# Attention's scores and values in four 64x64 tiles of the array, with two accumulators for the values

## The chip, the cores and the metric

The kernel runs on one core of a Trainium2 chip. The metric is the device time of one execution in microseconds (us). The kernel before has a median of 3139.4 us over three runs, from 3138.46 to 3145.35.

Engines are named as the profile names them: PE (TensorE, matmuls), PEld (its weight loads), DVE (VectorE), ACT (ScalarE), POOL (GpSimd) and SP (the queue that issues most transfers). All arithmetic is in float32.

## The reference, cut to what matters

An image batch x of shape (4, 128, 64, 64) passes through two layers. Layer 0 adds to x a group-normed block of three convolutions (7x7, 5x5, 3x3) and a non-local attention. Layer 1 is a two-way state-space block (mamba) and a recurrence. The change touches the attention of layer 0 only:

```python
g_x = conv1x1(x, gw, gb).reshape(B, IC, hw)      # IC = 64, hw = 4096
theta = conv1x1(x, tw, tb).reshape(B, IC, hw)
phi = conv1x1(x, pw, pb).reshape(B, IC, hw)
f = jnp.einsum('bcn,bcm->bnm', theta, phi) / jnp.sqrt(jnp.float32(IC))
attn = jax.nn.softmax(f, axis=-1)
out = jnp.einsum('bcm,bnm->bcn', g_x, attn)
out = conv1x1(out.reshape(B, IC, H, W), ow, ob)
```

Each of the four images has 4096 queries and 4096 keys of 64 channels.

## The kernel before, in words

`conv_attention` runs layer 0. It takes the queries in 32 tiles of 512 (eight for each image; `n` in the loop), and for each tile it does two things one after the other on PE: a chunk of attention, and a piece of the convolutions (`convolve`, whose matmuls are `products`, L367).

**The attention chunk.** The keys of an image are 32 blocks of 128, kept in pairs. `phi` holds channels of even blocks on partitions 0 to 63 and of odd blocks on 64 to 127; the queries `th` are held twice, once on each half. The loop over `i` has 8 steps of four key blocks. In a step:

- `scores` (L460, L462) takes two pairs. For each pair one PSUM tile `pf` of two banks is filled by two matmuls with 64 rows and 128 columns of the array, one for each half of the partitions (`HALF[e]`) into a bank of its own. ScalarE takes the exponential of both banks in one instruction into `ex` (four buffers).
- `values` (L471) multiplies each `ex` with the transposed `gT`: 128 rows, 64 columns, even blocks into the lower half of the accumulator `acc`, odd ones into the upper half. VectorE adds `ex` into `es` (L475, L477), for the denominators.

On PE the scores of step i+1 stand ahead of the values of step i, so a tile's order is two steps of scores, then values and scores in turn, then two steps of values. PE and ACT run in an order written out by hand; DVE, POOL and SP take their instructions in the order of dependencies that the program gives.

**After the chunk.** VectorE adds the two halves of `es` (L651). The convolution's first products go into PSUM tiles of the pool `ps_c`, which has three banks that go round, and are evicted by ACT (L410) and DVE (L414, L418, L420). After the first eviction comes `divide`: a matmul with ones gives the denominators `den` (L481), VectorE inverts them into `att` (L483), takes their extremes for a guard (L484, L485) and multiplies `acc` by them (L486). `collect` (L491, L493) projects finished tiles and adds them to the image. Before the convolution's last products `queries` (L449, L451) makes the next `th`, and the next tile's scores follow.

[...]

**Other work within the chunk.** `making_forms` prepares the convolution's inputs on POOL and ACT (L298, L337, L347); in the first two tiles `making` prepares the convolution's weights on VectorE (L537 to L582); `late` holds additions to the image on POOL (L388, L501). They are issued step by step between scores and values.

Of the kernel before, what the change touches and what calls it, by code (L numbers as in the profile page):

```python
# [10 lines left out]
F32 = mybir.dt.float32  # L11
AF = mybir.ActivationFunctionType
ALU = mybir.AluOpType
AX = mybir.AxisListType
PSUM = bass.MemoryType.PSUM

P = 128
NC = 512
# [130 lines left out]
def run(parts):  # L149
    for _ in parts:  # L150
        pass


def conv_attention(nc, tc, k, a, t, B, H, W, flags, load, mem, loads):
# [17 lines left out]
    NT = T // P  # L172
# [14 lines left out]
    with ExitStack() as ctx:  # L187
# [15 lines left out]
        HALF = [slice(0, IC), slice(IC, P)]  # L203
# [15 lines left out]
        wk = ctx.enter_context(tc.tile_pool(name="l0_wk", bufs=2))  # L219
# [4 lines left out]
        ps_v = ctx.enter_context(tc.tile_pool(name="l0_v", bufs=1, space=PSUM))  # L224
        ps_c = ctx.enter_context(tc.tile_pool(name="l0_c", bufs=3, space=PSUM))
# [7 lines left out]
        dmax = wp.tile([1, B * NQ], F32, name="dmax")  # L233
        dmin = wp.tile([1, B * NQ], F32, name="dmin")

        def statistics(b):

            st = wk.tile([P, NQ, nc.vector.BN_STATS_DIM], F32, tag="st", name="st")
            for j in range(NQ):
                nc.vector.bn_stats(st[:, j, :], t[:, ds(b * T + j * NC, NC)])  # L240
            mv = wk.tile([P, 2], F32, tag="mv", name="mv")
            nc.vector.bn_aggr(mv, st)
            pm = ps_c.tile([P, 1], F32, tag="c", name="pm")
            nc.tensor.matmul(pm, k.gmean, mv[:, 0:1], start=True, stop=True)
            gm = wk.tile([P, 1], F32, tag="gm", name="gm")
            nc.vector.tensor_copy(gm, pm)
            dm = wk.tile([P, 1], F32, tag="dm", name="dm")
            nc.vector.tensor_tensor(dm, mv[:, 0:1], gm, ALU.subtract)
            qv = wk.tile([P, 1], F32, tag="qv", name="qv")
            nc.vector.scalar_tensor_tensor(qv, dm, dm, mv[:, 1:2], ALU.mult, ALU.add)  # L250
            pv = ps_c.tile([P, 1], F32, tag="c", name="pv")
            nc.tensor.matmul(pv, k.gmean, qv, start=True, stop=True)
            ve = wk.tile([P, 1], F32, tag="ve", name="ve")
            nc.vector.tensor_scalar(ve, pv, GN_EPS, None, ALU.add)
            rs = wk.tile([P, 1], F32, tag="rs", name="rs")
            rsqrt(nc, k, rs, ve)
            return gm, rs
# [25 lines left out]
        def rows(b, r0, r1):  # L283

            nc.vector.tensor_scalar(
                xp[:, 3 + r0 : 3 + r1, 3 : 3 + W],
                t[:, ds(b * T + r0 * W, (r1 - r0) * W)].rearrange("p (h w) -> p h w", w=W),
                *gn[b], ALU.subtract, ALU.mult,
            )
# [80 lines left out]
        def fetch(m, n):  # L370
            wt = fm.tile([P, 9, P], F32, tag="wt", name="wt")
            nc.scalar.dma_start(wt, wd[3 * m + n])
            return wt
# [71 lines left out]
        def queries(n):  # L445
            b, q = divmod(n, NQ)
            pt = ps_c.tile([P, NC], F32, tag="c", name="pt")
            r = 3 + q * RW
            nc.tensor.matmul(pt, tw, xp[:, r : r + RW, 3 : 3 + W], start=True, stop=True)  # L449
            th = wk.tile([P, NC], F32, tag="theta", name="theta", bufs=1)  # L450
            nc.scalar.activation(th, pt, AF.Identity, bias=tb2)  # L451
            return th

        def scores(th, m0):

            out = []
            for m in range(2 * m0, 2 * m0 + 2):
                pf = ps_f.tile([P, 2, NC], F32, tag="f", name="pf")
                for e in range(2):
                    nc.tensor.matmul(pf[:, e, :], phi[HALF[e], m, :], th[HALF[e]], start=True, stop=True)  # L460
                ex = ep.tile([P, 2, NC], F32, tag="ex", name="ex")
                nc.scalar.activation(ex, pf, AF.Exp, scale=scale)  # L462
                out.append(ex)
            return out

        def values(m0, exs, acc, es):

            for i, ex in enumerate(exs):
                m = 2 * m0 + i
                for e in range(2):  # L470
                    nc.tensor.matmul(  # L471
                        acc[HALF[e]], gT[:, 2 * m + e, :], ex[:, e, :], start=(m == 0), stop=(m == NT // 2 - 1)
                    )
                if m == 1:
                    nc.vector.tensor_tensor(es, exs[0], ex, ALU.add)  # L475
                elif m > 1:
                    nc.vector.tensor_tensor(es, es, ex, ALU.add)  # L477

        def divide(n, acc, es):
            den = ps_c.tile([P, NC], F32, tag="c", name="den")  # L480
            nc.tensor.matmul(den, k.ones, es[:, 0, :], start=True, stop=True)  # L481
            att = wk.tile([P, NC], F32, tag="att", name="att", bufs=4)
            nc.vector.reciprocal(att, den)  # L483
            nc.vector.tensor_reduce(dmax[:, n : n + 1], att[0:1, :], AX.X, ALU.max)  # L484
            nc.vector.tensor_reduce(dmin[:, n : n + 1], att[0:1, :], AX.X, ALU.min)  # L485
            nc.vector.tensor_tensor(att, acc, att, ALU.mult)  # L486
            return att

        def collect(n, att):
# [105 lines left out]
        phi = big.tile([P, NT // 2, P], F32, name="phi")  # L595
        gT = big.tile([P, NT, IC], F32, name="gT")
        gn, mid, atts, xl, late, begun = {}, {}, {}, [], {}, set()
# [9 lines left out]
        def product(n):  # L607
            b, q = divmod(n, NQ)
            return (FIRST if b == 0 else ORDER if b + 1 < B else LAST)[q]

        th = None
        for j in range(T // XT):
            part = keys(0, j)
            next(part)
            if j == T // XT - 1:
                th = queries(0)
# [10 lines left out]
        for n in range(N):  # L627
            b, q = divmod(n, NQ)
            more = b + 1 < B and q == NQ - 1
            if 3 <= n < B + 2:  # L630
                load(n - 2)
            m, f, wts = product(n), nf, None
            if b + 1 < B and q == NQ - 3:
                gn[b + 1] = statistics(b + 1)
            if more:
                rows(b + 1, 0, H)
            acc = ps_v.tile([P, NC], F32, tag="v", name="acc")
            es = ep.tile([P, 2, NC], F32, tag="es", name="es", bufs=1)
            for i in range(NB):
                exs = nxt  # L640
                if i + 1 < NB:
                    nxt = scores(th, i + 1)
                values(i, exs, acc, es)
                next(making_forms, None)
                next(making, None)
                if m < 6 and i == NB - 3:
                    wts = [fetch(m, 0), fetch(m, 1)]
                due = late.get(n, [])
                for _ in range(-(-len(due) // (NB - i))):
                    due.pop(0)()  # L650
            nc.vector.tensor_tensor(es[:, 0, :], es[:, 0, :], es[:, 1, :], ALU.add)  # L651

            for i, _ in enumerate(convolve(n, b, m, f, wts)):
                if i == 0:

                    if q not in ((1, 2, 3) if b == 0 else (1,)):
                        for o in sorted(atts):
                            collect(o, atts.pop(o))
                    if q == 0 and n:
                        finish(b - 1)  # L660
                    if n == N - 1:
                        load_last()
                if i == 1:
                    atts[n] = divide(n, acc, es)
                if i == 2 and n + 1 < N:

                    nf = []
                    making_forms = forms(product(n + 1), nf)
                    next(making_forms, None)
                if more and i < T // XT:  # L670
                    part = keys(b + 1, i)
                    next(part)
                if i == 2 and n + 1 < N:
                    th = queries(n + 1)
                if i == 3 and n == NQ + 5:
                    mr = wk.tile([P, NT, 2], F32, tag="mr", name="mr", bufs=1)
                    stats = row_scales(nc, k, ps_c, "c", wk, t[:, 0:T], mr, mem)
                if i == 3 and n >= NQ + 5:
                    next(stats, None)
                if more and i < T // XT:  # L680
                    run(part)
                if i == 4 and n == N - 1:
                    collect(n, atts.pop(n))
                    finish_last(0)
            if n + 1 < N:
                nxt = scores(th, 0)
# [1070 lines left out]
```

## Time and profile before

| | us |
|---|---|
| median of three runs | 3139.4 |
| span of the profiled execution | 3147.0 |
| PE busy in it | 2925.4 |
| DVE busy | 2195.2 |
| ACT busy | 1813.8 |
| POOL busy | 1798.5 |
| L460 scores, PE, 2048 records | 513.6 |
| L471 values, PE, 2048 records | 492.8 |
| L477 additions to `es`, DVE, 448 | 683.2 (1.525 each) |
| L462 exponentials, ACT, 512 | 497.6 (1.021 each) |

The page gives the span, from the first instruction to the last, and no other time of that execution. Busy time is the time in which at least one record of a kind ran. PE's records overlap: the mean length of a score record is 0.619 us, while 513.6 us over 2048 records are 0.25 us each. So lengths of records say little about PE's pace, and one reads the distance from start to start instead. A line of the timeline gives the start, the length, the engine, the line, the operation with out<-in, rows*columns of the array, the shape and the count of merged records; in brackets stands the idle time before it and what ended it.

Attention and convolution take the stretch to about 1643 us; the granted clock of PE is 1.00 on average from 105 us to there, and 0.977 over the whole span, where it falls to half for stretches of 3.4 us and more.

### The profile page before, as it was taken

What the parts mean: (1) busy time and instruction counts of PE and PEld (TensorE: products, weight loads), DVE (VectorE), ACT (ScalarE), POOL (GpSimd) and SP (SyncE); (2) the same over time, 40 slices, a digit from 0 to 9 for tenths busy, and PEclk for the clock granted to TensorE, in tenths of its full rate; (3) what the DMA queues carried; (4) which work ended last, traced back from release to release, by engine and by line L of the source; (5) the groups of instructions that cost most, each with busy time, mean ns of one, the idle gap of its engine ahead of it and who ended that gap; (6) DMA issues with size and microseconds to landing.
All of it is one profiled execution on the core that took longest, in us unless ns stands there. A gap on an engine that the chain in (4) does not pass through costs nothing. (4 is left out here: it accounts for less than half of the span.)

```text
span 3147.0 us, 42863 instructions
## 1 busy us (share of the span) xinstructions
PE 2925.4 (93%) x15511; PEld 1458.2 (46%) x15511; DVE 2195.2 (70%) x3429; ACT 1813.8 (58%) x3102; POOL 1798.5 (57%) x1393
## 2 busy tenths in 40 slices
PE   6799999999999999999997999999999999999976
PEld 1344444454444454444453444444444444455545
DVE  7876668666777667687765767776677766777667
ACT  3343434433444434444434878887788778888756
POOL 4258448456584665766553565565555565565644
PEclk9999999999999999999998999999999999999988
DMA  5310101010100101010023343334333343333332
GB/s 181 133 39 30 38 31 45 8 43 23 46 23 30 43 23 38 31 52 33 11 74 92 91 117 95 98 95 115 82 100 94 80 120 89 105 95 103 87 109 109
DMA packets 108394, 224.16 MB, mean 71 GB/s; under 512 B 25678, under 2 KB 29390, under 8 KB 106764
## 3 DMA queue, kind: packets, MB, share of 16 engines
q1 hardware_dynamic: 96588, 177.53, 19.9%
q10 hardware_dynamic: 11584, 43.78, 4.1%
q8 instruction: 125, 2.05, 0.3%
q14 instruction: 97, 0.79, 0.1%
HBM read 200.83 MB, written 20.44 MB: 70 GB/s over the span
## 5 line engine op out<-in xcount | busy, mean ns | idle before, releaser
L477 DVE TENSOR_TENSOR es<-es,ex 128x1024 f32<-128x1024 f32 x448 | 683.2, 1525 | 139.2 <-ACT ex L462 105.8
L462 ACT ACTIVATE ex<-pf 128x1024 f32<-128x1024 f32 x512 | 497.6, 1021 | 464.7 <-PE pf L460 421.2
L460 PE MATMUL pf<-theta,phi 64*128 64x512 f32 x2048 | 513.6, 619 | 20.4 <-ACT ex L462 20.0
L471 PE MATMUL acc<-ex,gT 128*64 128x512 f32 x2048 | 492.8, 607 | 1.7 <-ACT ex L462 1.7
L1202 POOL TENSOR_TENSOR ct<-ct,Cst 128x512 f32<-128x512 f32 x128 | 170.7, 1334 | 343.6 <-DMA ct<-csmem 314.1
L460 PEld LDWEIGHTS pf<-theta,phi 64*128 64x128 f32 x2048 | 173.0, 185 | 340.0 <-ACT ex L462 172.3
L1168 ACT ACTIVATE lt<-lt,cs 128x128 f32<-128x128 f32 x1024 | 312.1, 390 | 0.5 <-DMA lt<-csmem 0.5
L367 PE MATMUL pm<-yf,wt 128*128 128x256 f32 x1152 | 287.1, 382 | 11.9 <-DVE att L483 11.0
L410 ACT ACTIVATE eo<-pm 128x256 f32<-128x256 f32 x88 | 33.7, 383 | 448.9 <-PE pm L367 442.3
L471 PEld LDWEIGHTS acc<-ex,gT 128*64 128x64 f32 x2048 | 127.9, 137 | 339.8 <-issue 327.8
L367 PEld LDWEIGHTS pm<-yf,wt 128*128 128x128 f32 x1152 | 212.9, 189 | 93.4 <-issue 38.7
L1103 PE MATMUL pb<-tl,wbc_fwd 128*64 128x512 f32 x512 | 241.9, 616 | 6.5 <-DVE xT L1135 6.5
L1103 PE MATMUL pb<-tl,wbc_bwd 128*64 128x512 f32 x512 | 242.5, 617 | 0.0
L337 POOL TENSOR_TENSOR yf<-yd 128x272 f32<-128x272 f32 x192 | 234.0, 1246 | 1.4
L1267 POOL TENSOR_TENSOR yT<-yT,zT 128x512 f32<-128x512 f32 x127 | 166.5, 1316 | 58.1 <-DVE yT L1254 50.0
L337 POOL TENSOR_TENSOR yf<-xp 128x272 f32<-128x272 f32 x128 | 108.7, 880 | 136.0 <-PE pm L367 130.2
L1201 DVE TENSOR_TENSOR lt<-lt,gm 128x1024 f32<-128x1024 f32 x128 | 179.2, 1400 | 1.9
L1135 DVE SCALAR_TENSOR_TENSOR xT<-px,taps_bwd,xT 128x512 f32<-128x512 f32 x192 | 143.7, 748 | 8.7 <-ACT xT L1129 4.0
L1234 PE MATMUL y<-lt,xdt 128*64 128x128 f32 x2048 | 142.3, 282 | 7.6 <-PE ptr L1177 3.8
L1221 POOL TENSOR_TENSOR S<-S,tot 128x256 f32<-128x256 f32 x120 | 91.4, 762 | 100.7 <-PE y L1242 91.2
L1103 PEld LDWEIGHTS pb<-tl,wbc_fwd 128*64 128x64 f32 x512 | 66.9, 141 | 174.3 <-issue 142.9
L367 PE MATMUL pm<-yf,wc 128*128 128x256 f32 x512 | 131.3, 384 | 6.6 <-DVE att L483 5.1
(297 smaller groups left out, 5655.5 us busy)
## 6 DMA issues: line engine op xcount, KB each, us to landing
lt<-csmem SPq DMA_DIRECT2D x128, 512.0 KB, 5.7
wt<-wd ACTq DMA_DIRECT2D x72, 576.0 KB, 3.8
ct<-csmem SPq DMA_DIRECT2D x256, 128.0 KB, 5.2
rs<-m SPq DMA_DIRECT2D x31, 512.0 KB, 3.8
wd<-t SPq DMA_DIRECT2D x16, 576.0 KB, 2.8
t<-in_x SPq DMA_DIRECT2D x4, 2048.0 KB, 11.0
rows<-after SPq DMA_DIRECT2D x32, 256.0 KB, 4.4
out<-t SPq DMA_DIRECT2D x4, 2048.0 KB, 14.4
```

The lines of the kernel that those rows point to most:

```text
L337: nc.gpsimd.tensor_tensor(f[:, kx], at(x), at(y), op)
L367: nc.tensor.matmul(pm[:, e, :], wt, src, start=(i == 0), stop=(i == len(terms) - 1))
L460: nc.tensor.matmul(pf[:, e, :], phi[HALF[e], m, :], th[HALF[e]], start=True, stop=True)
L462: nc.scalar.activation(ex, pf, AF.Exp, scale=scale)
L471: nc.tensor.matmul(acc[HALF[e]], gT[:, 2 * m + e, :], ex[:, e, :], start=(m == 0), stop=(m == NT // 2 - 1))
L477: nc.vector.tensor_tensor(es, es, ex, ALU.add)
L1103: nc.tensor.matmul(out, w[i]["bc"][:, tap, bass.ts(c, DS)], src, start=(tap == 0), stop=(tap == KC - 1),)
L1135: nc.vector.scalar_tensor_tensor(at(n), px, taps[:, PAD - n : KC - n], at(n), ALU.mult, ALU.add)
L1168: nc.scalar.activation(v, v, AF.Relu, scale=-1.0, bias=m["b"]["cs"][:, d, m["i"], h : h + 1])
L1201: nc.vector.tensor_tensor(lt, lt, gm.unsqueeze(2).to_broadcast([P, ND, NHEAD, P]), ALU.mult)
L1202: nc.gpsimd.tensor_tensor(m["ct"], m["ct"], Cs[:, cols].unsqueeze(1).to_broadcast([P, NHEAD, P]), ALU.mult)
L1267: eng.tensor_tensor(v, v, gr["z"][d][:, :, half(d, j // 2)], ALU.mult)
```

## The change

The scores' matmuls are split by output: each of the two becomes two of 64 rows and 64 columns, one for each half of the keys in a block (`c`), so that four matmuls fill `pf` on the four quarters of the array.

The values' matmuls are split by operand: the lower and the upper half of a key block's partitions (`r`) go into different accumulators, `acc[0]` in `ps_v` and `acc[1]`, a new tile in one of the three banks of `ps_c`. Both are held for the whole chunk. At its end ScalarE copies `acc[1]` to `att` in SBUF and VectorE adds `acc[0]` to it. `divide` gets this sum; it puts the inverted denominators into the second half of `es`, which is free by then.

```diff
-                for e in range(2):
-                    nc.tensor.matmul(pf[:, e, :], phi[HALF[e], m, :], th[HALF[e]], start=True, stop=True)
+                for c in HALF:
+                    for e in range(2):
+                        nc.tensor.matmul(pf[c, e, :], phi[HALF[e], m, c], th[HALF[e]], start=True, stop=True)
...
                 for e in range(2):
-                    nc.tensor.matmul(
-                        acc[HALF[e]], gT[:, 2 * m + e, :], ex[:, e, :], start=(m == 0), stop=(m == NT // 2 - 1)
-                    )
+                    for r in range(2):
+                        nc.tensor.matmul(
+                            acc[r][HALF[e]], gT[HALF[r], 2 * m + e, :], ex[HALF[r], e, :],
+                            start=(m == 0), stop=(m == NT // 2 - 1),
+                        )
...
-        def divide(n, acc, es):
+        def divide(n, att, es):
             den = ps_c.tile([P, NC], F32, tag="c", name="den")
             nc.tensor.matmul(den, k.ones, es[:, 0, :], start=True, stop=True)
-            att = wk.tile([P, NC], F32, tag="att", name="att", bufs=4)
-            nc.vector.reciprocal(att, den)
-            nc.vector.tensor_reduce(dmax[:, n : n + 1], att[0:1, :], AX.X, ALU.max)
-            nc.vector.tensor_reduce(dmin[:, n : n + 1], att[0:1, :], AX.X, ALU.min)
-            nc.vector.tensor_tensor(att, acc, att, ALU.mult)
+            r = es[:, 1, :]
+            nc.vector.reciprocal(r, den)
+            nc.vector.tensor_reduce(dmax[:, n : n + 1], r[0:1], AX.X, ALU.max)
+            nc.vector.tensor_reduce(dmin[:, n : n + 1], r[0:1], AX.X, ALU.min)
+            nc.vector.tensor_tensor(att, att, r, ALU.mult)
             return att
...
-            acc = ps_v.tile([P, NC], F32, tag="v", name="acc")
+            acc = [ps_v.tile([P, NC], F32, tag="v", name="acc"), ps_c.tile([P, NC], F32, tag="c", name="acc2")]
...
             nc.vector.tensor_tensor(es[:, 0, :], es[:, 0, :], es[:, 1, :], ALU.add)
+            att = wk.tile([P, NC], F32, tag="att", name="att", bufs=4)
+            nc.scalar.copy(att, acc[1])
+            nc.vector.tensor_tensor(att, acc[0], att, ALU.add)
...
-                    atts[n] = divide(n, acc, es)
+                    atts[n] = divide(n, att, es)
```

## The prediction

> **What bounds the kernel now.** I read the page's totals first, then busy time by stretch, then the timeline of single query tiles. Attention and the convolution that is woven into it run to about 1643 us; the change touches nothing after that.
>
> ```profile
> PE 2925.4 (93%) x15511; PEld 1458.2 (46%) x15511; DVE 2195.2 (70%) x3429; ACT 1813.8 (58%) x3102; POOL 1798.5 (57%) x1393
> 105.00:1643.00 1538.00, 1494.15 (x6278) 701.57 (x6275) 1075.36 (x1022) 647.86 (x766) 926.49 (x670) 1.00 0.11 36
> ```
>
> The second line's fields are stretch, length, busy time of PE, PEld, DVE, ACT, POOL, then granted clock, DMA share and GB/s. PE is busy 1494 of 1538 us at full clock. No other engine is near that, so a tile of queries is paced by PE, and what counts is how PE spends its time. The timeline of one tile (start, length, engine, line, operation) shows it:
>
> ```profile
> 613.90 1.94 PE L471 MATMUL acc<-ex,gT 128*64 128x512 f32 x8
> 615.76 1.99 PE L460 MATMUL pf<-theta,phi 64*128 64x512 f32 x8
> 617.68 1.94 PE L471 MATMUL acc<-ex,gT 128*64 128x512 f32 x8
> 619.55 1.99 PE L460 MATMUL pf<-theta,phi 64*128 64x512 f32 x8
> ...
> 615.76 0.30 PEld L460 LDWEIGHTS pf<-theta,phi 64*128 64x128 f32 x4 [0.81 <-ACT ex L462]
> 616.30 0.19 PEld L460 LDWEIGHTS pf<-theta,phi 64*128 64x128 f32 x2 [0.24 <-issue]
> 616.73 0.19 PEld L460 LDWEIGHTS pf<-theta,phi 64*128 64x128 f32 x2 [0.23 <-issue]
> ```
>
> One f32 matmul is two records here (1024 score matmuls in the code, 2048 records), call them passes. Records come in pairs, one per half of the array, 7 ns apart, so both halves work at once. The eight records of a group are four pairs: they start at 615.76, 616.30, 616.73 and (in the unmerged records) 617.16, and the next group at 617.68. The regular step is 0.43 us. Four steps are 1.72 us, but a score group takes 1.92 and a value group 1.87. The excess is at the borders only: a score group's second pair comes 0.103 late (its weights start to load with the first matmul) and the value group 0.092 late; a value group's second pair comes 0.050 late and the next score group 0.095 late. The array's shape changes there, 64x128 to 128x64 and back.
>
> Whether the shape is to blame is told by borders where only the line changes. Den to convolution (both 128x128) is 602.33 to 603.19, exactly two steps:
>
> ```profile
> 602.33 1.02 PE L481 MATMUL den<-es,ones 128*128 128x512 f32 x2
> 603.19 1.89 PE L367 MATMUL pm<-yf,wc 128*128 128x256 f32 x8
> ```
>
> Over the whole trace, borders between lines of one shape have a typical excess of 1 to 3 ns where nothing is waited for (31 from L1115 to L1146, 23 from L491 to L367); borders between shapes have 92 to 97 ns everywhere, in the mamba stage too.
>
> **The change part by part.**
>
> *Borders.* Scores and values now both use 64x64. In a tile of queries there are 8 borders from scores to values and 7 back (the first two score groups and last two value groups are adjacent). A score-to-value border costs 0.092 + 0.050 = 0.142, a value-to-score border 0.095 + 0.103 = 0.198: 8 x 0.142 + 7 x 0.198 = 2.52 us. The entry from the convolution into the scores stays a change of shape, but its late second pair costs 0.051 with 64 columns of weights (the L1242 group below: first to second four 0.160 against a step of 0.109) and not 0.103: 0.05 more. That is **2.57 us a tile**. The exit stays.
>
> *Four tiles in place of two.* Each matmul becomes two of half the size, 1024 more matmuls for scores and 1024 for values; the multiplications are the same, so if four tiles run together at the step of 0.43 the groups stay 1.72 us. Fours exist in this trace, in the mamba stage, with the same nesting (output half outside, operand half inside) and two banks:
>
> ```profile
> 2027.65 1.09 PE L1234 MATMUL y<-lt,xdt 128*64 128x128 f32 x16
> 2028.67 0.67 PE L1242 MATMUL y<-ct,S 64*64 64x128 f32 x16
> 2029.27 0.33 PE L1187 MATMUL small<-ident,Bst 128*128 128x128 f32 x1
> ```
>
> Sixteen records in twos take 1.02 us to the next start, sixteen in fours 0.60. In the records the fours start 7 ns apart within and 0.109 us from four to four: the step of one full 128-column pass (L1177: 0.109). Their weight loads are issued 7 ns apart and lie under the running pass.
>
> Here I weigh a rule that speaks against the change: the Trainium skill, "TensorE: Matmul & The Clock Gate", section "Measured speedup vs the span model", gives 3.07x for four row tiles at 512 columns, not 4x. By it a group of 0.86 us (one 128-key pair, two passes) would take 0.86 x 4 / 3.07 = 1.12, an estimate; 32 groups a tile x 30 tiles x 0.26 = 250 us lost. By the row, 0. I take the row: it is this chip, this data type, streams of fours back to back and not one isolated pack. It has 128 columns where the change has 512, which is what could still speak for the rule.
>
> *The second accumulator* takes one of three "c" banks from the tile's start to the copy. The banks go round, so the third tile taken after it (second or third of the convolution, which PE reaches 1.7 to 2.7 us after the chunk or later) needs that bank; the copy is done some 0.9 us after the chunk. No cost. PE's first values of the next tile wait for a bank used three allocations earlier, read long before, since 4.2 us of scores come first.
>
> *The copy on ScalarE* (nearest row L451, 128x512 out of PSUM, 0.69 us) waits for the last values. Behind it on that queue stands L410, which waits for the first products until 2.0 us after the chunk. Hidden; uncovered it would be 0.69 x 32 = 22 us.
>
> *The addition on VectorE* (L486, 128x512 with an operand in PSUM: 0.67 us) waits for the copy; behind it stand the L414 evictions. In a tile such as 609.7 VectorE ends L651 0.68 after the chunk and then idles 1.76 us for ScalarE, which hides it. The division afterwards is the same five instructions on other buffers: 0. Nothing on the SP or POOL queue moves.
>
> *VectorE's tail.* The chunk now ends 2.57 us earlier, but the 15 additions of es do not get shorter; where they trail, they trail more. I replayed each tile's VectorE durations against exponentials brought forward, with 0.7 for the new addition. In 18 of the 30 tiles the first L414 does not move. In twelve it comes 0.3 to 2.3 us later, in most of them into VectorE's idle time before the reciprocal. It gets through to PE in four. The worst tile is shown (chunk ends at 1499.8):
>
> ```profile
> 1500.07 4.31 DVE L477 TENSOR_TENSOR es<-es,ex 128x1024 f32<-128x1024 f32 x2
> 1504.42 0.69 DVE L651 TENSOR_TENSOR es<-es 128x512 f32<-128x512 f32 x1
> 1505.03 0.88 DVE L414 SCALAR_TENSOR_TENSOR eo<-pm,eo 128x256 f32<-128x256 f32 x2
> ...
> 1507.19 3.36 DVE L483 RECIPROCAL att<-den 128x512 f32<-128x512 f32 x1
> ```
>
> There VectorE has no gap left, so the reciprocal, whose end frees the bank that PE wants next, moves by 2.4 us; in the tiles that end at 954.3, 549.3 and 1357.0 by 0.9, 0.4, 0.1. Sum 3.8.
>
> *The first two tiles* (loops of 43.3 and 34.2 us against 30.5) are paced by VectorE, which prepares weights between the additions: exponentials wait 33.9 us for it. No gain, and 0.7 us in the first tile, where VectorE is 15 us behind.
>
> *Sum:* 30 x 2.57 = 77.2 saved, 3.8 + 0.7 = 4.5 given back: **-72.7 us**. The profiled span of 3147.0 becomes 3074.3. The page gives no time around the span; the span is 7.6 us above the median of the runs (1.65 above the slowest), about the worth of four or five of its 3.4 us half-clock stretches. Taken from the median: 3139.4 - 72.7 = **3067**.
>
> **The rivals.**
>
> *VectorE becomes the bound* (0.13). For: additions take 1.24 us in the tile at 664.9, where POOL is light, and 2.0 in that at 1469.3; 15 of the latter, 30 us, outlast a chunk of 27.95. Against: four exponential buffers let it trail, and 18 tiles have room. If the 11 tiles with a mean of 1.6 us or more gain nothing and pay the new addition, 11 x 3.27 = 36 us go: 3139.4 - 77.2 + 0.7 + 36 = 3099.
>
> *Four tiles don't stream at the full rate with 512 columns* (0.12, the slower side). Place: every step of L460 and L471; price by the rule above: -77 + 250 + 4.5 = +177, so 3317. It decides from 72.7 us / (30 tiles x 64 steps) = 38 ns a step: at 0.468 in place of 0.430 all is lost. The same holds if the passes don't interleave over the four tiles or if each step shows its 51 ns of weight load (+25, so 3165). Against: L1242.
>
> *The borders don't belong to the shape* (0.03): data or semaphores cause them and they remain; about 3144, if the addition is hidden. Against: 92 to 97 ns at every change of shape, 1 to 3 without.
>
> **How the numbers follow.** The likeliest case (0.72) gives 3067, its own range 3055 to 3080 (half-clock stretches come and go, and the tail is replayed, not measured). With the VectorE rival at 3099 the range becomes 3050 to 3105. What a measurement can tell from no change is 0.2%, 6 us. Faster: 0.72 + 0.13 = 0.85; same 0.03; slower 0.12.
>
> **What would show it.** In the profile after, a score or value group of the chunk should be 1.72 us from start to start (now 1.92 and 1.87), in fours 0.43 apart; an undisturbed chunk 27.95 us (now 30.52); the first two tiles unchanged; PEld no longer starting with the group's first matmul; VectorE's waits for exponentials (105.8 us) much smaller. A step above 0.43 would show the rate rival, PE waiting for es or for exponentials the VectorE rival. I am wrong if quarter tiles with 512 columns behave unlike those with 128, or if the granted clock drops when four tiles run, which no row here shows for long stretches.

## The result and the profile after

The changed kernel has a median of 3096.07 us over four runs (3092.08 to 3096.92), the kernel before 3139.65 beside it. The ratio is 0.9854, with a 95% interval from 0.984 to 0.9868: 43.6 us less, where 72.7 had been forecast. A repetition later gave 3098.27. The profiled span is 3093.7 us.

The page's totals and the groups that changed (line, engine, operation, count, then busy time and mean ns of one, then idle time before them):

```profile
PE 2858.4 (92%) x19607; PEld 1461.9 (47%) x19607; DVE 2245.6 (73%) x3461; ACT 1834.4 (59%) x3134; POOL 1812.9 (59%) x1393
L480 DVE TENSOR_TENSOR es<-es,ex 128x1024 f32<-128x1024 f32 x448 | 703.0, 1569 | 83.6 <-ACT ex L463 43.2
L461 PE MATMUL pf<-theta,phi 64*64 64x512 f32 x4096 | 496.7, 599 | 19.2 <-ACT ex L463 18.8
```

PE's busy time fell by 67.0 us and the span by 53.3: some of what the multiplications gave became idle time. VectorE waits 43.2 us for exponentials where it waited 105.8; the same line before was

```profile
L477 DVE TENSOR_TENSOR es<-es,ex 128x1024 f32<-128x1024 f32 x448 | 683.2, 1525 | 139.2 <-ACT ex L462 105.8
```

The gain itself is plain in the timeline of a tile, first PE, then its weight loads:

```profile
607.07 1.90 PE L473 MATMUL acc<-ex,gT 64*64 64x512 f32 x16
608.79 1.90 PE L461 MATMUL pf<-theta,phi 64*64 64x512 f32 x16
610.51 1.90 PE L473 MATMUL acc<-ex,gT 64*64 64x512 f32 x16
612.22 1.90 PE L461 MATMUL pf<-theta,phi 64*64 64x512 f32 x16
```

```profile
608.36 0.15 PEld L461 LDWEIGHTS pf<-theta,phi 64*64 64x64 f32 x4 [0.28 <-ACT ex L463]
608.79 0.15 PEld L461 LDWEIGHTS pf<-theta,phi 64*64 64x64 f32 x4 [0.28 <-issue]
609.22 0.15 PEld L461 LDWEIGHTS pf<-theta,phi 64*64 64x64 f32 x4 [0.28 <-issue]
```

Every group is 1.72 us from start to start (they were 1.92 and 1.87), the fours are 0.43 apart, and the scores' first weights are loaded at 608.36, a step ahead of the group at 608.79. An undisturbed chunk, from its first scores to the convolution's first multiplication, takes 28.20 us after 30.52.

What became of the rest is told by stretches, read from the starts of PE's first records in each. Tile 0 and 1 run from the first scores of one tile to those of the next. From tile 2 on each tile is divided in two: its chunk, and its convolution stretch, from the convolution's first multiplication to the next tile's first scores.

| us | before | after | forecast |
|---|---|---|---|
| tile 0 | 68.4 | 83.1 | +0.7 |
| tile 1 | 46.1 | 40.9 | 0 |
| chunks of tiles 2 to 31 | 925.8 | 859.2 (-66.7) | -77.2 |
| convolution of tiles 2 to 30 | 566.2 | 579.2 (+12.9) | +3.8 |
| end of the last chunk, from the span's start | 1642.4 | 1597.3 (-45.1) | -72.7 |

Three terms are off: the chunks by 10.5 us, the first two tiles by 8.9 (9.6 more instead of 0.7), the convolution by 9.1; the first scores came 1.0 earlier. Behind attention, where no instruction was changed, the profiled spans differ by another 8.2 us. Two profiled executions of the changed kernel differ there by 4.2 us (1496.4 and 1500.6), and the time at half clock is 123 us before and 115 after, so this part is no gain of the change; the medians' 43.6 is close to attention's 45.1.

### The profile page after: what moved, and what is told of

Its sections match the earlier page's. It is cut to its first block, busy times and chain, and to the rows that moved or that the text cites. A ratio compares the mean times of both kernels' runs of the same rounds, so it can differ in the third digit from the quotient of the medians.

```text
span 3093.7 us, 51126 instructions
## 1 busy us (share of the span) xinstructions
PE 2858.4 (92%) x19607; PEld 1461.9 (47%) x19607; DVE 2245.6 (73%) x3461; ACT 1834.4 (59%) x3134; POOL 1812.9 (59%) x1393
## 3 DMA queue, kind: packets, MB, share of 16 engines
q8 instruction: 157, 2.57, 0.4%
## 5 line engine op out<-in xcount | busy, mean ns | idle before, releaser
L480 DVE TENSOR_TENSOR es<-es,ex 128x1024 f32<-128x1024 f32 x448 | 703.0, 1569 | 83.6 <-ACT ex L463 43.2
L461 PE MATMUL pf<-theta,phi 64*64 64x512 f32 x4096 | 496.7, 599 | 19.2 <-ACT ex L463 18.8
L473 PE MATMUL acc<-ex,gT 64*64 64x512 f32 x4096 | 486.7, 596 | 7.9 <-ACT ex L463 7.9
L473 PEld LDWEIGHTS acc<-ex,gT 64*64 64x64 f32 x4096 | 158.5, 135 | 298.2 <-issue 286.5
L461 PEld LDWEIGHTS pf<-theta,phi 64*64 64x64 f32 x4096 | 147.3, 133 | 311.7 <-issue 212.7
L337 POOL TENSOR_TENSOR yf<-xp 128x272 f32<-128x272 f32 x128 | 119.0, 961 | 97.4 <-PE pm L367 91.6
```

What stands on the lines that cost most here:

```text
L337: nc.gpsimd.tensor_tensor(f[:, kx], at(x), at(y), op)
L461: nc.tensor.matmul(pf[c, e, :], phi[HALF[e], m, c], th[HALF[e]], start=True, stop=True)
L473: nc.tensor.matmul(acc[r][HALF[e]], gT[HALF[r], 2 * m + e, :], ex[HALF[r], e, :], start=(m == 0), stop=(m == NT // 2 - 1),)
```

## The experiments

Three questions: is the shape border the whole gain; why do the first tiles lose; why do the convolution stretches lose, with the multiplications in them unchanged? Times are medians; each ratio is to the kernel before, timed on the same chip, with its 95% interval.

### One half of the change at a time

scores_only splits the scores and leaves the values, with one accumulator, as before; values_only is the reverse. The diff is that from the changed kernel to values_only; scores_only keeps these lines and takes everything else of the change back:

```diff
-                for c in HALF:
-                    for e in range(2):
-                        nc.tensor.matmul(pf[c, e, :], phi[HALF[e], m, c], th[HALF[e]], start=True, stop=True)
+                for e in range(2):
+                    nc.tensor.matmul(pf[:, e, :], phi[HALF[e], m, :], th[HALF[e]], start=True, stop=True)
```

> Scores in four 64x64 tiles, values as before in two 128x64 tiles with one accumulator. Theory (the change of the array's shape at the borders is what costs): the shape still changes at every border, so nothing of the border's 92 to 97 ns goes; only the second fours of a score group come 0.05 late in place of 0.10 (eight times a tile). A score group 1.86 us from start to start (was 1.92), a value group 1.87 as before, an undisturbed chunk 30.1 us (was 30.52), the whole some 12 us faster, about 3127. Rival (quarter tiles are faster in themselves, each half of the change brings its half): chunk about 29.4, the whole 22 us or more faster.

> Values in four 64x64 tiles with two accumulators, the copy and the addition; scores as before in two 64x128 tiles. Theory (shape): the shape still changes at every border: score group 1.92, value group 1.87, an undisturbed chunk 30.5. The costs of the second accumulator are paid without any gain: VectorE's queue in the first tile of queries is ordered as in the changed kernel (weights' work and the next image's statistics ahead), some 14 us, and the division's multiplication is slow beside POOL, 5 us: about 3155 to 3160, slower than before. Rival (quarter tiles are faster in themselves): chunk about 29.4, and the whole not slower than before.

Measured: 3127.93 (0.9971, 0.9961 to 0.9982) and 3162.63 (1.008, 1.0063 to 1.0097). PE in scores_only, and in values_only:

```profile
613.95 1.94 PE L472 MATMUL acc<-ex,gT 128*64 128x512 f32 x8
615.82 1.95 PE L461 MATMUL pf<-theta,phi 64*64 64x512 f32 x16
617.70 1.94 PE L472 MATMUL acc<-ex,gT 128*64 128x512 f32 x8
```

```profile
626.23 1.99 PE L460 MATMUL pf<-theta,phi 64*128 64x512 f32 x8
628.15 1.95 PE L472 MATMUL acc<-ex,gT 64*64 64x512 f32 x16
630.03 1.99 PE L460 MATMUL pf<-theta,phi 64*128 64x512 f32 x8
```

With one half alone the border stays: groups of 1.87 and 1.88 here, of 1.92 and 1.88 there, chunks of 30.22 and 30.59 where they were 30.52. The scores' half alone saves 0.30 us a chunk, the values' half alone costs 0.07; together they give 2.32. So it is the equal shape that pays, not the smaller tiles. In scores_only the two kinds differ in rows alone (64 and 128), in values_only in columns alone, and a border of either sort keeps its excess of about 0.09 us. And the losses belong to the values' half: tile 0 takes 68.5 us in scores_only and 81.9 in values_only, the convolution stretches 566.3 and 574.6.

### The sum left in PSUM

VectorE's multiplication of the division had one operand in PSUM and one in SBUF before; after the change both are in SBUF. psum_sum writes the sum of the accumulators back into `acc[0]`:

```diff
-            nc.vector.tensor_tensor(att, acc[0], att, ALU.add)
+            nc.vector.tensor_tensor(acc[0], acc[0], att, ALU.add)
...
-            nc.vector.tensor_tensor(att, att, r, ALU.mult)
+            nc.vector.tensor_tensor(att, acc, r, ALU.mult)
```

> As the changed kernel, but the sum of the accumulators is written back into the first accumulator in PSUM, so that the multiplication of the division reads PSUM and SBUF and not SBUF twice. Theory (two SBUF operands make VectorE slow while POOL runs): all 32 multiplications 0.67 to 0.69 us (now 18 of 32 take 1.5 to 1.96), the convolution stretches of the tiles 3, 14, 16, 22 and 25 get back their 0.6 to 1.05 us, the whole about 5 us faster than the changed kernel, 3091. Rival (the slow multiplication is hidden and those stretches are longer for the addition's sake): multiplications shorter, stretches and time unchanged, 3096.

Measured: 3092.15 (0.9848, 0.9831 to 0.9864). The number of slow multiplications in the changed kernel is 16 of 32, not 18. The durations view (shortest, median, longest ns; first and last start) of this one instruction before, after, and in psum_sum:

```profile
L486 DVE TENSOR_TENSOR att<-acc,att x32: 668/669/693, 102.1 to 1653.7; 128x512 f32<-128x512 f32 x32
```

```profile
L489 DVE TENSOR_TENSOR att<-att,es x32: 668/1094/1957, 115.2 to 1608.3; 128x512 f32<-128x512 f32 x32
```

```profile
L489 DVE TENSOR_TENSOR att<-acc,es x32: 668/669/670, 113.9 to 1602.7; 128x512 f32<-128x512 f32 x32
```

The slow 16, of 1.52 to 1.96 us, are those beside which POOL runs for 95% of the time or more; the other 16 (POOL at most 23%) take 0.67. With the operand in PSUM all 32 take 0.67, 16 of them under a POOL that runs throughout. How it reaches PE is seen in tile 3 after the change, on VectorE, on POOL, and on PE:

```profile
241.82 1.76 DVE L489 TENSOR_TENSOR att<-att,es 128x512 f32<-128x512 f32 x1
243.51 0.42 DVE L414 SCALAR_TENSOR_TENSOR eo<-pm,eo 128x256 f32<-128x256 f32 x1
```

```profile
240.52 2.52 POOL L298 TENSOR_TENSOR yx<-yx,xp 128x1190 f32<-128x1190 f32 x1 [23.21 <-ACT yx L301]
243.12 3.03 POOL L298 TENSOR_TENSOR yx<-yx,yb 128x1190 f32<-128x1190 f32 x1
```

```profile
242.81 0.61 PE L367 MATMUL pm<-yd,wt 128*128 128x256 f32 x2
244.19 2.61 PE L367 MATMUL pm<-yf,wt 128*128 128x256 f32 x11 [0.76 <-DVE eo L414]
```

and, in psum_sum, on PE:

```profile
241.92 2.75 PE L367 MATMUL pm<-yf,wt 128*128 128x256 f32 x12
```

POOL's instruction ends at 240.52 + 2.52 = 243.04, the multiplication at 243.58, 0.54 later. All 16 slow multiplications end 0.54 or 0.55 us after the end of the POOL instruction that ran when they started. POOL's next one takes 3.03 where the same takes 2.70 in psum_sum. That is the picture that the Trainium skill gives ("SBUF — State Buffer", section "Who interferes with whom"): a VectorE instruction with two SBUF inputs and a GpSimd instruction that reads SBUF share one read interface, and the second to come blocks until the first is done. PE's stall of 0.76 us is missing in psum_sum, and the stretch of tile 3 is 16.20, 17.20, 16.20 us before, after and in psum_sum; tiles 14, 22 and 25 go the same way (18.22, 19.27, 18.21; 17.17, 18.09, 17.17; 16.20, 17.17, 16.38).

Yet the sum over all stretches falls by 1.6 us only (579.2 to 577.6): tiles 9, 17, 26 and 28 get longer by 0.2 to 1.0 each, for a reason that was not followed up. The instruction's price is shown; a gain in the whole time is not, the intervals of the two kernels overlap.

### VectorE's order in the first tiles

VectorE's order comes from the program, and the changed kernel has another one in tile 0 than the kernel before. Its timeline there, then PE's:

```profile
78.17 1.36 DVE L581 SCALAR_TENSOR_TENSOR t<-t 128x1152 f32<-128x1152 f32 x1 [9.51 <-POOL t L574]
79.44 1.22 DVE L480 TENSOR_TENSOR es<-es,ex 128x1024 f32<-128x1024 f32 x1
...
106.24 1.29 DVE L240 BATCH_NORM_STATS2 st<-t 128x6 f32<-128x512 f32 x2 [7.07 <-DMA t<-in_x]
107.44 0.41 DVE L414 SCALAR_TENSOR_TENSOR eo<-pm,eo 128x256 f32<-128x256 f32 x1
```

```profile
81.83 1.99 PE L473 MATMUL acc<-ex,gT 64*64 64x512 f32 x8 [7.50 <-ACT ex L463]
98.71 2.05 PE L484 MATMUL den<-es,ones 128*128 128x512 f32 x2 [7.32 <-DVE es L654]
108.92 3.75 PE L367 MATMUL pm<-yf,wc 128*128 128x256 f32 x8 [8.16 <-DVE eo L414]
```

Twice VectorE stands, that is, the first instruction of its queue waits and all behind it wait too: 9.51 us for a sum of weights that POOL has not finished (L581, ahead of additions whose exponentials are there), and 7.07 for the transfer of the next image, whose statistics (L240) come ahead of an eviction. PE is idle for 7.50 and 8.16 us behind the two. Before, the stand for the weights was 2.51 us (the line is L578 there), and L240 came in tile 1:

```profile
79.47 2.63 DVE L578 SCALAR_TENSOR_TENSOR t<-t 128x1152 f32<-128x1152 f32 x2 [2.51 <-POOL t L571]
108.29 3.66 DVE L240 BATCH_NORM_STATS2 st<-t 128x6 f32<-128x512 f32 x6 [3.23 <-DMA t<-in_x]
```

The kernel before had an idle time of its own in tile 0: PE waited 10.98 us for the denominators there, and 7.32 after.

Two kernels set only VectorE's order of issue and add no wait: pin_stats puts the statistics behind tile 0's division, pin_tile0 also puts the second half of the making of weights (what the program states from step 15 on, with eight steps to a tile) behind the tenth addition of tile 0. The first edit is in both, the second in pin_tile0 alone:

```diff
-                gn[b + 1] = statistics(b + 1)
+                with tc.issue_after(first[0]) if b == 0 else ExitStack():
+                    gn[b + 1] = statistics(b + 1)
...
-                next(making, None)
+                with tc.issue_after(adds[9]) if n * NB + i > 14 else ExitStack():
+                    next(making, None)
```

> As the changed kernel, but in the first tile of queries VectorE's queue is held to about the order of the kernel before: the second half of the weights' sums behind ten additions of es, and the next image's statistics behind the division. The arithmetic is the same. Theory (the first tile loses 14.7 us because VectorE's queue was ordered anew and stands twice at its head for POOL and for a transfer): from the first scores to those of the second tile 69 us (now 83.1, before 68.4), the whole some 14 us faster than the changed kernel, about 3082. Rival (the loss is the half clock, or comes of the copy and the addition in the first tile): still 78 us or more, time 3090 to 3097.

> As the changed kernel, but with the next image's statistics behind the division of the first tile; the weights' sums stay where the changed kernel has them. It tells the two stands of VectorE in the first tile apart. Theory: the wait of 7.1 us for the transfer goes, that of 9.5 us for POOL stays: from the first scores to those of the second tile about 75 us (changed kernel 83.1, pin_tile0 71.6); the statistics then fall into the second tile (pin_tile0: 45.1 against 40.9), so the whole moves by only 3 to 5 us, to about 3092. Rival (POOL's wait makes nearly all of the loss): 80 us or more.

Measured: 3087.78 (0.9834, 0.9818 to 0.9851) and 3089.27 (0.9843, 0.9824 to 0.9861). Tile 0 falls to 71.6 and 72.8, but tile 1 rises from 40.9 to 45.1 and 44.1: the statistics now fall there. Order is the cause of most of tile 0's loss (83.1, and 68.4 before), but a third of the remedy is given back in tile 1. Nearly all of the remedy is the statistics': in pin_stats the stand of 9.51 us is still there, and taking it away as well brings another 1.2 us only, since PE then waits longer for the denominators (11.91 us, and 6.78 in pin_stats). The whole comes to -8 and -7 us by the medians, for pin_tile0 less than expected, and the intervals overlap with the changed kernel's, so these two times alone would not settle it.

### The additions of the accumulators, later

After the change L414, the convolution's eviction, comes late also in tiles 7, 15, 23 and 26 (each stretch 0.8 to 1.0 longer than before). In tile 7 the chunk ends at 440.96:

```profile
441.65 2.25 DVE L262 TENSOR_SCALAR xn<-t,gm,rs 128x1024 f32<-128x1024 f32 x3
443.82 0.68 DVE L657 TENSOR_TENSOR att<-acc,att 128x512 f32<-128x512 f32 x1
444.42 0.87 DVE L414 SCALAR_TENSOR_TENSOR eo<-pm,eo 128x256 f32<-128x256 f32 x2
```

The new addition stands between other work and the evictions. late_pin is psum_sum with that addition moved behind the reciprocal:

```diff
+            inv = nc.vector.reciprocal(r, den).ins
+            with tc.issue_after(inv):
+                nc.vector.tensor_tensor(acc, acc, att, ALU.add)
```

> As psum_sum, and the addition of the two accumulators issued on VectorE behind the reciprocal and not ahead of the convolution's first evictions. Theory (where VectorE trails at the end of a chunk, the addition's 0.7 us goes through to PE): the convolution stretches of the tiles 7, 15 and 23 fall from 30.1 to 29.3, those of 9, 17, 26 and 28 by about 0.7 each; the whole 4 to 5 us less than psum_sum, about 3088. Rival (the trailing additions of es alone delay PE, and the addition behind the reciprocal costs the same there): stretches as in psum_sum, 3092.

Measured: 3096.03 (0.9869, 0.9851 to 0.9887), a miss. Against psum_sum, tiles 7, 15 and 23 fall from 30.1 to 29.5 us and tile 28 from 18.07 to 14.83, the direction expected, but tile 14 goes from 18.21 to 21.44, tile 6 from 17.06 to 18.01, tile 22 from 17.17 to 18.01. All stretches of the convolution together gain 3.3 us and the chunks lose 2.4. Tile 14 shows what can happen; VectorE and PE in late_pin:

```profile
789.93 2.39 DVE L285 TENSOR_SCALAR xp<-t,gm,rs 128x4096 f32<-128x4096 f32 x1
792.25 0.41 DVE L414 SCALAR_TENSOR_TENSOR eo<-pm,eo 128x256 f32<-128x256 f32 x1
```

```profile
792.76 4.51 PE L367 MATMUL pm<-yf,wt 128*128 128x256 f32 x12 [2.02 <-issue]
```

In psum_sum both evictions of this tile's middle stand ahead of the long L285; with the addition moved, the second falls behind it. PE is idle for 2.02 us, and then its twelve records take 4.51 us, beside a clock of one half from 793.6 on for 3.4 us. In best2 (below), which has the same order here, the same idle time comes without the half clock, the twelve records take 2.83, and the tile 19.75. So of the 3.2 us about 1.7 are the clock. The clock has a like share in tile 28, where psum_sum has a half-clock stretch of 3.4 us and late_pin none (PE's idle time falls by 1.57 of the 3.24), and in the 2.4 us of the chunks: in tile 4, the only chunk that differs much (33.59 and 35.92), half clock lasts 3.4 and 6.8 us. Tiles 6 and 22 were not pursued.

### Weights and statistics later still

before_defer (from the kernel before) and best2 (from late_pin) put the making of weights behind tile 0's division and the statistics there too:

```diff
-                next(making, None)
+                with tc.issue_after(done[0].ins) if n * NB + i > 14 else ExitStack():
+                    next(making, None)
```

> The kernel before, with VectorE's queue held in the first tile: the second half of the weights' sums and the next image's statistics behind the division of the first tile. No matmul is changed. Theory (PE waits 11 us for the denominators of the first tile, behind weights' sums that nobody needs yet): from the first scores to those of the third tile about 105 us (now 114.4), the whole 8 to 10 us faster than before, about 3130. Rival (VectorE's work in the first two tiles has to be done there and only moves into the second tile): 112 us or more, time within 3 us of before.

> late_pin and the order of before_defer together: scores and values in four tiles, sum in PSUM behind the reciprocal, weights' sums and statistics behind the first tile's division. If the causes add up: from the first scores to those of the third tile about 105 us (changed kernel 124.0), convolution stretches as in late_pin, the whole about 3070, which is near the predicted 3067. If the first tile is bound by VectorE's work whatever its order: 3085 to 3090.

Measured: 3143.49 (1.0016, 1.0005 to 1.0028) and 3091.46 (0.9851, 0.9833 to 0.9869). Both miss. Tile 0 falls to 56.7 us in both, but tile 1 takes 60.8 and 65.5. VectorE and PE in best2:

```profile
122.18 3.07 DVE L240 BATCH_NORM_STATS2 st<-t 128x6 f32<-128x512 f32 x5 [9.69 <-DMA t<-in_x]
```

```profile
127.55 3.71 PE L461 MATMUL pf<-theta,phi 64*64 64x512 f32 x16 [11.07 <-ACT ex L463]
```

VectorE comes earlier to the statistics than the transfer does: the stand has moved, not gone. best3 (from psum_sum) and before3 (from the kernel before) keep this hold on the weights and put the statistics of all later images behind the third tile's division; best4 is best3 with the weights behind the tenth addition instead.

```diff
-                gn[b + 1] = statistics(b + 1)
+                with tc.issue_after(first[0]):
+                    gn[b + 1] = statistics(b + 1)
...
+                    if n == 2:
+                        first.append(done[-1].ins)
```

> psum_sum with the second half of the weights' sums behind the first tile's division, as in best2, and the statistics of all later images behind the third tile's division. Theory (in best2 the statistics only carried the stand for the transfer into the second tile; put where the image has long landed, they cost their 15 us of VectorE once): first scores to third tile's scores about 98 to 101 us (changed kernel 124.0, best2 122.2), some 5 us more in tiles 2 and 3, the whole about 3075. Rival (VectorE's work at the start is the bound whatever its order): 3088 or more.

> The kernel before with the same two holds on VectorE's queue and no other change. It tells how much of best3 is the order and how much the four tiles. Theory: first scores to third tile's scores about 101 to 103 us (before 114.4), some 5 us back in tiles 2 and 3, about 3130; best3 stays 55 us ahead of it (30 tiles x 2.32 = 70 less about 13 in the convolution stretches).

> psum_sum with the weights' sums in the first tile held as in pin_tile0 (behind ten additions) and the statistics of later images behind the third tile's division. Theory: first tile 71 us as in pin_tile0, second 40 (no statistics in it), together 111; the whole about 3083. Rival (the weights' sums are better in the first tile, where PE waits anyway, than in the second): not slower than best3.

> The changed kernel once more, on the same chip as best3 and before3, for the comparison: 3096 within 0.2%, the first tile 83 us, the chunk 28.20.

Measured: best3 3074.63 (0.9788, 0.9765 to 0.9811), before3 3125.40 (0.9953, 0.9935 to 0.9971), best4 3079.75 (0.9804, 0.9785 to 0.9823), the changed kernel again 3098.27 (0.986, 0.9835 to 0.9885). VectorE in tile 0 of best3 has no stand left:

```profile
64.40 19.60 DVE L480 TENSOR_TENSOR es<-es,ex 128x1024 f32<-128x1024 f32 x8
84.03 0.69 DVE L658 TENSOR_TENSOR es<-es 128x512 f32<-128x512 f32 x1
84.64 0.69 DVE L662 TENSOR_TENSOR acc<-acc,att 128x512 f32<-128x512 f32 x1
85.24 0.87 DVE L414 SCALAR_TENSOR_TENSOR eo<-pm,eo 128x256 f32<-128x256 f32 x2
```

Tiles 0 and 1 together: 114.4 us before, 124.0 after, 99.7 in before3, 99.6 in best3. The order alone is worth 16 us to the kernel before (3141.69 to 3125.40 on this chip) and, in best3, which also has psum_sum's edit, 24 to the changed one. With the same order in those tiles, what remains of the change (best3 against before3) is 3125.40 - 3074.63 = 51 us: the chunks of tiles 2 to 31 are 63.0 us shorter, the convolution stretches 7.6 longer. best3 is faster than both kernels of this study.

## Why the prediction was right and wrong

**Right: what pays, and its unit prices.** The shape borders were the gain: they vanish only when both lines have one shape (2.32 us a chunk against 0.30 and -0.07 with one half). With the order of the first tiles set alike and the sum left in PSUM (best3 against before3) the change is worth 51 us, of 72.7 forecast. The rival that the borders don't belong to the shape falls.

**Right: four tiles run at full rate.** With 512 columns too the fours are 0.430 apart, all through the chunks. The Trainium skill's 3.07x ("TensorE: Matmul & The Clock Gate", "Measured speedup vs the span model") is for four row tiles of 32 rows each, which no run here has; it does not carry over to these back-to-back streams of 64x64 tiles, which take the step of one full 128x128 pass: 4.0 of 4. To go by the row L1242 and not by that figure was right.

**Wrong in size: the count of borders, "8 x 0.142 + 7 x 0.198".** The order in a tile is S0 S1 V0 S2 V1 S3 V2 and so on to S7 V6 V7. Scores go over to values ahead of V0 to V6, 7 times, and values to scores ahead of S2 to S7, 6 times. The trace before has 224 and 192 of them in its 32 tiles. That gives 7 x 0.142 + 6 x 0.198 + 0.05 = 2.23, and 2.32 was measured; with 2.57 I had 0.25 too much in each of 30 chunks, 7.5 us. Undisturbed chunks are 26 of 30 and give 60.3; the other four (tiles 4, 5, 13 and 21) leave the sum 2.9 short of 30 x 2.32. Half clock fell into tiles 5 and 13 of them before and into 4, 5 and 21 after.

**Wrong: "The first two tiles ... No gain, and 0.7 us".** I took VectorE's order there as given, and it is not: with the values' half of the change, whose new instructions for VectorE stand at the end of the chunk, the program came to another order well before them (values_only has the same loss, scores_only has none). Two stands of 9.51 and 7.07 us came of it. The granted clock from 0 to 105 us is 0.85 after and 0.93 before; half-clock stretches begin in tile 0 at 49.8, 70.3, 77.1 and 94.2 us (before: 71.8 and 88.8) and fill 41.0 us of the first two tiles (before: 13.7; best3: 10.2). How much of the loss is the clock's own no run separates; the order is the cause of the idle times, which are gone in best3.

**Wrong: "The division afterwards is the same five instructions on other buffers: 0".** The buffers were the point. One operand moved from PSUM to SBUF, and 16 multiplications of 0.67 us became 1.52 to 1.96. This accounts for most of the roughly 1 us that each of tiles 3, 14, 22 and 25 lost, as psum_sum shows (tile 25 keeps 0.18 of its 0.97).

**The right tiles, in part for other reasons: VectorE's tail, "Sum 3.8".** Tile 28 (the one ending at 1499.8) was to lose 2.4 and lost 3.49; the tiles ending at 954.3, 549.3 and 1357.0 (17, 9 and 25) were to lose 0.9, 0.4 and 0.1 and lost 0.39, 0.37 and 0.97, the last by its slow multiplication. After the change the chunk of tile 28 ends at 1458.22:

```profile
1455.09 7.94 DVE L480 TENSOR_TENSOR es<-es,ex 128x1024 f32<-128x1024 f32 x4
1463.06 1.64 DVE L654 TENSOR_TENSOR es<-es 128x512 f32<-128x512 f32 x1
1464.63 0.68 DVE L657 TENSOR_TENSOR att<-acc,att 128x512 f32<-128x512 f32 x1
1465.23 0.87 DVE L414 SCALAR_TENSOR_TENSOR eo<-pm,eo 128x256 f32<-128x256 f32 x2
```

```profile
1466.24 1.94 PE L484 MATMUL den<-es,ones 128*128 128x512 f32 x2 [2.50 <-DVE eo L414]
1467.98 2.78 PE L367 MATMUL pm<-yf,wc 128*128 128x256 f32 x8
```

```profile
1466.40:1469.70 3.30, 3.30 (x7) 1.91 (x7) 2.36 (x3) 0.00 (x0) 1.29 (x1) 0.50 0.00 0
```

The last line has the fields of the prediction's second line; its clock is 0.50. The additions of `es`, which were to trail more, end 4.81 us after the chunk, and before 4.55. L414 comes 1.81 later, of which 0.26 are theirs, 0.60 the new addition's and 0.95 those of L654, the sum of the two halves of `es`: it too has both operands in SBUF, and beside POOL it takes 1.64 where it took 0.69. In tiles 9 and 17 it goes from 0.69 to 1.67. PE's idle time grows by 1.80 (from 0.70), and the remaining 1.69 are a half-clock stretch of 3.4 us behind it, for which the prediction has no term; best3, without one there, takes 15.28 for this stretch. That the forecast of 2.4 is near is luck. Not in the sum at all were tiles 7, 15, 23 (0.83 to 0.85) and 26 (0.98), where the new addition queues behind other work with the evictions behind it. I replayed VectorE's durations and took the cover of "0.68 after the chunk and then idles 1.76" from one tile; three tiles of an image border have none.

**Right: the copy on ScalarE, the bank.** No wait of PE for a bank of the second accumulator appears in an undisturbed chunk. The copy takes 0.586 us; PE waits for it once, for 0.7 us, so nearly all of its 32 x 0.586 us is hidden from PE. VectorE waits for it in seven tiles, 3.8 us in all.

**The rival that VectorE becomes the bound** gave 3099, close to the 3096 measured, but for another reason: it had the chunks of 11 tiles gaining nothing, and all 26 undisturbed ones of 30 gained in full. VectorE took its share at the ends of chunks and in tile 0. The likeliest case's own range, 3055 to 3080, does not hold the result; it lies within 3050 to 3105 only because this rival had widened the range, and that is luck as far as the cause goes.

## What to carry to other kernels

Where two kinds of multiplications alternate on TensorE, compare their array shapes: each change of shape cost about 0.1 us here, plus the weights loaded late, and splitting both kinds to one shape removed it at no cost in rate; splitting one alone left it. Before costing an edit to "the same instructions", look at where each operand now lives, and compare, before and after, the order of instructions on every engine whose queue the program orders by itself, also far from the edit. When a stand at the head of a queue is taken away, look for what the engine reaches too early next: here the wait for one transfer moved from the first tile to the second until the work that needs it was put behind the third.

## What the hardware showed that was not expected

- A multiplication of 128x512 on VectorE with both operands in SBUF took 0.67 us alone and 1.52 to 1.96 beside a running POOL; with one operand in PSUM it took 0.67 under a POOL that ran throughout. An addition with both operands in SBUF (L654) took 0.68 to 0.69 alone and 1.01 to 1.67 in the 18 of 32 that POOL delayed, while the addition of the accumulators, one of them in PSUM (L657), took 0.68 to 0.69 in all 32. The additions to `es` (both operands in SBUF, 128x1024) took 1.22 us on average without POOL and 1.70 where POOL ran throughout.
- From 105 us to the end of attention each stretch of half clock, two before and four after, began when PE had been idle for 1.5 to 2.7 of the 3.4 us ahead of it. So an idle time of PE can cost more than its length: 1.80 us more of it in tile 28 lengthened the stretch by 3.49. Not each one does: in best3 the 2.42 us there are not followed by half clock, and what decides it is not shown.
- A border between tiles of different shape costs about 0.09 us on PE whether rows or columns differ. A change of line without a change of shape showed no excess within the chunk: four to four is 0.430 there too.
